# A vision tower's mixture-of-experts and linear-attention stages: GpSimd's order fixed by hand among the expert blocks and in the first attention units

## The chip, the cores and the metric

The kernel runs on one core of a Trainium2 chip. A core has a tensor engine for matrix products (PE, whose weight loads are a row of their own, PEld), a vector engine (DVE), a scalar engine (ACT), GpSimd (POOL) and a sync engine (SP) that issues most DMA transfers. Each engine executes its own list of instructions in order, and waits on semaphores for the others. The metric is the device time of one execution in microseconds, lower is better.

## The reference

The program is a two-layer transformer tower on 4 images. A tokenizer makes 784 tokens of 256 features from 8 x 8 patches, and three equal copies of them, so 3136 distinct tokens are computed and the output is written three times. Layer 0 has an attention across images and then a mixture of six experts, of which each token takes two:

```python
top_w, top_i = jax.lax.top_k(expert_logits, TOP_K)
routing_weights = jax.nn.softmax(top_w, axis=-1)
...
combined = jnp.sum(sel * routing_weights[..., None], axis=2)
```

Layer 1 has a linear attention. Its q and k come from normalised rows, and its sums run over all tokens of an image:

```python
k2 = _l2_normalize(k2 / (k2s + EPS_DIV), axis=-2)
q2 = _l2_normalize(q2 / (q2s + EPS_DIV), axis=-1)
kv = jnp.einsum('bnc,bnd->bcd', k2, v)
t2 = jnp.einsum('bnc,bcd->bnd', q2, kv) / math.sqrt(N)
attn = v + t2
return attn @ W_out + b_out
```

A second mixture of four experts ends the layer. Between the parts stand residual adds and layer norms.

## The kernel before, in words

The 3136 tokens lie as 25 tiles of 128 rows in a resident array `h`: six tiles for each image, and one last tile that holds the 16 remaining tokens of all four images (the remainder).

**Expert blocks.** The router has given every token two rows in a DRAM array, sorted by expert. The experts run over 30 blocks of 256 such rows: load a block, transpose it on PE, two hidden layers (`hidden`), the output layer (`rows_back`), and a write to the DRAM array `yrows`. Seven early blocks run beside the attention of layer 0; the loop at L1629 runs the other 23. A token's two results are fetched back from `yrows` by indirect DMAs on GpSimd, the gathers (`fetch`, L1531, the issue is L1540): one gather takes one of the two rows of each of 128 tokens, 128 KB.

**Units.** The linear attention works on units of three tiles: units 0 to 7, two for each image, and unit 8, `LU`, the remainder, with one tile. So `fetch` issues six gathers for a unit and two for the remainder. The gathered rows land in a buffer `ys`; units 0 to 7 share three buffers, and the remainder has one of its own. For each tile `stats_one` (L1548) adds the two rows, weighted, into `h` (L1554, two instructions) and takes mean and variance (`bn_stats` and `bn_aggr`, L1563 and L1564). Then `norm_root` (ACT) and `norm_rows` (DVE, L1585 and L1588) write the normalised rows `xa`, `x_t` transposes them on PE (L277), `qk_mm` makes q and k on PE (L1770), `qk_add` adds the bias (DVE, L1776), `qk_squares` takes the sums of squares (ACT), `root` and `factors` (DVE, L1808, L1809 and L1812) make the scales, `q_rows` (DVE, L1824) and `k_rows` (ACT, L1817) apply them, and `q_t` transposes q (PE, L277). When both units of an image are there, `k_x_tiles` (PE, L1869) and `k_x_left` (PE, L1876) sum k times x over the image's tiles and its part of the remainder, which is cut out of the remainder's normalised rows `xaL` into `xaM` by four GpSimd products (L1992). `rows_out` makes the output rows.

**What sets the order.** The kernel is written with a tile framework whose planner lays down each engine's list at build time. It goes by its own estimate of when an instruction's inputs will be there, and gives priority to what was written earlier. Inside a `manual_schedule` block the engines that are named keep the order in which the block is written. Instructions written outside the block may still be put between those of the block where the planner sees a gap. Before the change the block loop (L1627) fixes DVE and SP, and the block with the first units (L1974) fixes DVE, PE and ACT (`by_hand`); GpSimd is left to the planner in both. After the second block a loop over units 3 to 9 (L2055) is left to the planner altogether; there `q_k` (L1787) calls `stats_one` for the unit after the one whose q and k it makes. In the block loop the gathers of unit 0, unit 1, the remainder and unit 2 are written behind the block after which their rows are complete. Those of units 3, 4 and 5 are written in the second block, and the loop writes those of the unit three further on.

Of the kernel before, what the change touches and what calls it, by code (L numbers as in the profile page):

```python
# [65 lines left out]
def tile_vit_tower(ctx: ExitStack, tc: tile.TileContext, a: dict, out: bass.AP):  # L66
# [571 lines left out]
    ENG = mybir.EngineType  # L638
    by_hand = {ENG.DVE, ENG.PE, ENG.Activation}
# [575 lines left out]
    with tc.manual_schedule(engines=by_hand):  # L1215
        for s in range(NI - 1):
            u = (s - 1, 0, TPI) if s else None
# [62 lines left out]
    def load(i):  # L1280
        if i >= NBLK:
            return
        row = rowof[i] = nc.sync.value_load(meta(0, i), min_val=0, max_val=DUMMY)
        x = inT[i] = work[0].tile([P, 2, D], F32, tag="xb", name="xb", bufs=4)
        get = nc.sync.dma_start(
            out=x, in_=xrows[bass.ds(row, BLK), :].rearrange("(t p) d -> p t d", p=P)
        )
        if i < NEARLY:

            tc.declare_no_dep(get.ins, group="late scatter", reason="distinct rows")  # L1290
            tc.add_to_no_dep_group("early block", get.ins)
        for name in scatters[: scattered if i < NEARLY else None]:
            tc.add_manual_dep(
                get.ins, name,
                mybir.DependencyInfo(
                    mybir.DependencyClass.Sync, mybir.DependencyReason.DATA
                ),
                reason="rows scattered",
            )

    def own_weights(i):
        if i >= NBLK:
            return
        off = nc.vector.value_load(meta(1, i), min_val=0, max_val=(E0 - 1) * EW)
        w = own[i] = work[0].tile([P, EW], F32, tag="own", name="own", bufs=3)
        nc.vector.tensor_copy(w, ewf[0][:, bass.ds(off, EW)])  # L1306

    def turned(i):
        if i >= NBLK:
            return  # L1310
        x = inT.pop(i)
        pt = ps_tile("ptb").rearrange("p (c n) -> p c n", c=2)
        for c in range(2):
            for t in range(2):
                nc.tensor.transpose(  # L1315
                    pt[:, c, t * P : (t + 1) * P], x[:, t, c * P : (c + 1) * P], ident
                )
        xT = inT[i] = work[0].tile([P, 2, BLK], F32, tag="xTb", name="xTb")
        nc.scalar.copy(xT, pt)  # L1319

    def hidden(i, k):
        w = own[i]
        src = inT.pop(i) if k == 0 else h1s.pop(i)
        wm = w[:, k * 2 * D : (k + 1) * 2 * D].rearrange("p (c n) -> p c n", c=2)
        dst = work[0].tile([P, 2, BLK], F32, tag=f"hb{k}", name=f"hb{k}")
        for o in range(2):
            pm = ps_tile("pb")[:, :BLK]
            for c in range(2):
                nc.tensor.matmul(  # L1329
                    pm, wm[:, c, o * P : (o + 1) * P], src[:, c, :],  # L1330
                    start=(c == 0), stop=(c == 1),
                )
            b = w[:, 6 * D + 2 * k + o : 6 * D + 2 * k + o + 1]
            if o == 0 or i < NEARLY:
                nc.scalar.activation(dst[:, o, :], pm, AF.Relu, bias=b)  # L1335
            else:
                nc.vector.tensor_scalar(dst[:, o, :], pm, b, 0.0, ALU.add, ALU.max)  # L1337
        (hid2 if k else h1s)[i] = dst
# [25 lines left out]
    past, u, ua, ub = (s - 2, 0, TPI), (s - 1, 0, TPI), (s, 0, GT), (s, GT, TPI + 1 - GT)  # L1364
# [142 lines left out]
    LU = len(units)  # L1507
# [23 lines left out]
    def fetch(u):  # L1531

        if u >= len(units):
            return
        b, j0, n = units[u]
        y = ys[u] = own_of(lina, u, [TT, UT, 2, D], "ys", 3)
        for j in range(n):
            for k in range(2):
                t = b * TPI + j0 + j
                got = nc.gpsimd.indirect_dma_start(  # L1540
                    out=y[:, j, k, :], out_offset=None, in_=yrows[:, :],
                    in_offset=bass.IndirectOffsetOnAxis(ap=pos[:, k, t : t + 1], axis=0),
                )
                tc.add_to_no_dep_group("fetched", got.ins)
# [21 lines left out]
    def normalise(u):  # L1566
        norm_root(u)
        norm_rows(u)
# [55 lines left out]
        after[u] = NEARLY + most - 1  # L1624
    after[LU] = after[2] = NBLK - 1
    assert after[0] < after[1] < NBLK - 1
    with tc.manual_schedule(engines={mybir.EngineType.DVE, mybir.EngineType.SP}):  # L1627
        own_weights(NEARLY)
        turned(NEARLY)  # L1629
        for i in range(NEARLY, NBLK + 1):  # L1630
            if i < NBLK:
                load(i + 3)
                hidden(i, 0)
            rows_back(i - 1)
            own_weights(i + 1)
            turned(i + 1)
            if i < NBLK:
                hidden(i, 1)
            if i == NEARLY + 1:
                centred_weights()  # L1640
            for u in (0, 1, LU, 2):
                if i - 1 == after[u]:
                    fetch(u)

            for u, wait, two in ((0, 4, 1), (1, 4, 1)):
                j = (i - 1 - after[u] - wait) * two
                for k in range(j, j + two):
                    if 0 <= k < units[u][2]:
                        stats_one(u, k)
                    elif k == units[u][2]:  # L1650
                        normalise(u)
            if i - 1 == after[0] + 10:
                x_t(0)
# [317 lines left out]

    squares = {}
    steps = layer1_weights()
    with tc.manual_schedule(engines=by_hand):  # L1974
        x_t(1)
        for j in range(UT):
            qk_mm(0, j)
            qk_add(0, j)
            qk_squares(0, j)
        root(0)  # L1980
        for j in range(UT):
            qk_mm(1, j)
        qk_add(1, 0)
        qk_squares(1, 0)
        stats_one(LU, 0)
        norm_root(LU)
        factors(0)
        qk_add(1, 1)
        qk_squares(1, 1)
        norm_rows(LU)  # L1990
        for b in range(NI):
            nc.gpsimd.tensor_scalar(  # L1992
                xaM[:, b, :], xaL[:, 0, : D + 2], ofimage[:, b : b + 1], None, ALU.mult
            )
        fetch(3)
        fetch(4)
        qk_add(1, 2)
        qk_squares(1, 2)
        root(1)
        q_rows(0)  # L2000
        next(steps)
        x_t(LU)
        q_t(0)
        k_rows(0)
        next(steps)
        stats_one(2, 0)
        factors(1)
        q_rows(1)
        k_rows(1)
        qk_mm(LU, 0)  # L2010
        next(steps)
        Wvo, bvo = lw[:2]
        q_t(1)
        qk_add(LU, 0)
        qk_squares(LU, 0)
        root(LU)
        stats_one(2, 1)
        stats_one(2, 2)
        fetch(5)
        norm_root(2)  # L2020
        squares[0] = k_squares(0)
        factors(LU)
        fold(0, squares.pop(0))
        norm_rows(2)
        k_rows(LU)
        squares[LU] = k_squares(LU)
        q_rows(LU)
        squares[1] = k_squares(1)
        fold(1, squares.pop(1))
        k_x_tiles(0)  # L2030
        x_t(2)
        k_x_left(0)
        kn = k_norm(0)
        k_x_out(0, kn)
        qk_mm(2, 0)
        qk_add(2, 0)
        qk_squares(2, 0)
        stats_one(3, 0)
        qk_mm(2, 1)
        qk_add(2, 1)  # L2040
        qk_squares(2, 1)
        q_t(LU)
        gT = g_t(0)
        stats_one(3, 1)
        qk_mm(2, 2)
        qk_add(2, 2)
        kv_out(0, gT)
        qk_squares(2, 2)
        stats_one(3, 2)
        normalise(3)  # L2050
        rows_out(0)
        x_t(3)
    squares[2] = scales(2)
    fold(2, squares.pop(2))
    for u in range(3, LU + 2):  # L2055
        b, odd = divmod(u - 2, 2)
        one_image = not odd
        if u < LU:
            fetch(u + 3)
        if u == LU:  # L2060
            shared = shared1(0)
        if one_image:
            k_x(b)
            q_t(u - 1)
        if u < LU:
            q_k(u, 0, 2)
        if one_image:
            gT = g_t(b)
        if u < LU:
            q_k(u, 2, UT)  # L2070
            squares[u] = scales(u)
        if one_image:
            kv_out(b, gT)
        if u == LU - 1:
            rows_in(0)
            turn_rows(0)
            gate(0)
        if u < LU - 1:
            x_t(u + 1)
        if u == 3:  # L2080
            for k in pending:
                residual(k)
            pending = None
        rows_out(u - 2)
        if u == LU + 1:
            rows_left()
        if u < LU:
            fold(u, squares.pop(u))
            if u % 2:
                q_t(u - 1)  # L2090
# [103 lines left out]
```

## Time and profile before

| what | value |
|---|---|
| time, median of 3 runs | 788.0 us (787.89 to 788.85) |
| profiled execution: time, span | 788.72 us, 787.0 us |
| PE busy | 716.8 us, 91% of the span |
| DVE busy | 483.3 us, 61% |
| ACT busy | 331.8 us, 42% |
| POOL busy | 128.5 us, 16%, 226 instructions |
| gathers (L1540) | 52, mean 988 ns |
| xaM products (L1992) | 4, mean 1000 ns |
| mean granted PE clock | 0.962 |

Times in the trace are counted from the start of the span. The block loop ends at about 469 us, the block with the first units runs to about 540, and the loop over units from 3 on to about 620. The page shows each engine's busy time, the span in 40 slices, the chain of work that ended last, and the costliest groups of instructions with the idle time before them and what ended it. The trace can be asked for a table by stretch, for the waits, and for any engine's instructions in order of time. A row of such a timeline gives start, duration, engine, line, operation, output and inputs, and in brackets how long the engine had been idle and what released it.

### The profile page before, as it was taken

The page shows a single profiled execution, that of the slowest core. Times are in us where ns is not written, and L with a number is a line of the kernel's source. Part 1 is how long each engine was busy: PE and PEld are TensorE (multiplying, and loading weights), DVE is VectorE, ACT ScalarE, POOL GpSimd, SP SyncE. Part 2 cuts the span into 40 slices and gives each one's busy share as a digit, 9 for nine tenths or more (in the row PEclk, how much of TensorE's full clock was granted, in tenths as well). Part 3 has the DMA queues.
Part 4 walks back from the last instruction along what each step waited for, and adds up shares of the span by engine and source line. Part 5 has one row for each costly group of instructions (what it writes and reads, how often), then busy time and mean ns, then how long its engine had stood idle before and what let it go on. Part 6 is the DMA issues. An engine that isn't in the chain of part 4 may idle for free.

```text
span 787.0 us, 10609 instructions
## 1 busy us (share of the span) xinstructions
PE 716.8 (91%) x3408; PEld 495.9 (63%) x3408; DVE 483.3 (61%) x1515; ACT 331.8 (42%) x777; POOL 128.5 (16%) x226
## 2 busy tenths in 40 slices
PE   6899899999888789999999997379999999999996
PEld 4746555665555568878888883347776775554653
DVE  4676786769778745464456654579965654444441
ACT  0555776555574653422223225135445613222221
POOL 5300000000155127300113007860000000000000
PEclk9999999999999789999999999579999999999999
DMA  8399999000021944423344243230000003223333
GB/s 199 104 418 416 419 415 396 2 0 1 7 75 51 305 165 154 132 95 104 97 131 127 89 128 95 82 92 1 1 0 1 1 21 96 75 65 106 104 104 111
DMA packets 57749, 98.07 MB, mean 125 GB/s; under 512 B 6407, under 2 KB 47598, under 8 KB 57694
## 3 DMA queue, kind: packets, MB, share of 16 engines
q1 hardware_dynamic: 51184, 80.96, 29.4%
q0 software_dynamic: 5632, 14.58, 6.1%
q10 hardware_dynamic: 878, 1.86, 1.0%
q8 instruction: 27, 0.44, 0.2%
q14 instruction: 28, 0.23, 0.1%
HBM read 31.50 MB, written 65.88 MB: 124 GB/s over the span
## 4 chain that ended last, share of the span: by engine, by line
PE 70%; DVE 14%; ACT 5%; DMA 5%; POOL 3%; issue 2%; SPq 1%; DVEq 0%; ACTq 0%; POOLq 0%
PE pb L1329 13%; PE pyb L1346 6%; PE pe L286 6%; PE pqk L1770 5%; PE ps L286 4%; PE pt L277 4%; PE pkv L286 4%; PE pw L552 3%; PE pwp L297 3%; PE ps L2144 3%; PE pout L1944 3%; PE pout L1949 3%; PE pukx L1869 2%; DVE prod L815 2%; PE pe L2114 2%
## 5 line engine op out<-in xcount | busy, mean ns | idle before, releaser
L1039 POOL DMA_INDIRECT xrows<-xn,pos x50 | 54.6, 1091 | 242.4 <-ACT kq L790 186.2
L1540 POOL DMA_INDIRECT ys<-yrows,pos x52 | 51.4, 988 | 145.8 <-DMA yrows<-yb 131.0
L1329 PE MATMUL pb<-xTb,own 128*128 128x256 f32 x240 | 59.0, 390 | 3.4 <-DVE r L899 1.8
L1335 ACT ACTIVATE hb<-pb,own 128x256 f32<-128x256 f32 x74 | 35.0, 473 | 55.0 <-PE pb L1329 48.3
L1329 PE MATMUL pb<-hb,own 128*128 128x256 f32 x240 | 57.1, 380 | 0.3 <-DVE hb L1337 0.3
L1346 PE MATMUL pyb<-own,hb 128*128 128x256 f32 x240 | 57.1, 380 | 0.0
L1329 PEld LDWEIGHTS pb<-xTb,own 128*128 128x128 f32 x240 | 44.8, 195 | 11.6 <-issue 1.9
L1346 PEld LDWEIGHTS pyb<-own,hb 128*128 128x128 f32 x240 | 45.5, 190 | 6.3 <-DVE hb L1337 0.2
L1329 PEld LDWEIGHTS pb<-hb,own 128*128 128x128 f32 x240 | 43.5, 191 | 5.8 <-DVE hb L1337 0.7
L1770 PE MATMUL pqk<-Wqkv,lxT 128*128 128x512 f32 x100 | 46.9, 616 | 0.2 <-ACT lxT L86 0.2
L277 PE MATMUL pt<-ident,xn 128*128 128x128 f32 x200 | 34.5, 301 | 12.6 <-DVE xn L578 6.6
L286 PE MATMUL pe<-xT,eW 128*128 128x512 f32 (+1 forms) x112 | 46.0, 554 | 0.0
L1352 DVE TENSOR_TENSOR yb<-pyb,eb 128x512 f32<-128x512 f32 x30 | 20.7, 691 | 40.7 <-PE pyb L1346 40.7
L1319 ACT COPY xTb<-ptb 128x512 f32<-128x512 f32 x30 | 17.5, 583 | 63.4 <-PE ptb L1315 63.4
L277 PEld LDWEIGHTS pt<-ident,xn 128*128 128x128 f32 x200 | 25.3, 150 | 28.3 <-ACT xn L913 8.8
L552 PE MATMUL pw<-Wall,pT 128*128 128x512 f32 x96 | 42.6, 594 | 0.0
L1337 DVE TENSOR_SCALAR hb<-pb,own 128x256 f32<-128x256 f32 x46 | 22.2, 482 | 28.7 <-PE pb L1329 28.6
L1554 DVE SCALAR_TENSOR_TENSOR h<-ys,wk,h 128x256 f32<-128x256 f32 x50 | 23.5, 484 | 17.7 <-DMA ys<-yrows,pos 17.3
L815 DVE SCALAR_TENSOR_TENSOR prod<-kq 128x784 f32<-128x784 f32 x32 | 30.4, 972 | 6.0 <-ACT kq L1173 3.4
L286 PEld LDWEIGHTS pe<-xT,eW 128*128 128x128 f32 x112 | 20.3, 190 | 21.5 <-issue 16.5
L1784 ACT ACTIVATE qk<-qk 128x256 f32<-128x256 f32 x50 | 20.4, 408 | 28.4 <-DVE qk L1776 26.0
L1306 DVE COPY own<-ew 128x1540 f32 x30 | 29.0, 968 | 5.1 <-issue 1.6
(398 smaller groups left out, 1467.7 us busy)
## 6 DMA issues: line engine op xcount, KB each, us to landing
xrows<-nothing SPq DMA_DIRECT2D x22, 896.0 KB
yrows<-nothing SPq DMA_DIRECT2D x22, 896.0 KB
out_dram<-h SPq DMA_DIRECT2D x23, 384.0 KB
xb<-xrows SPq DMA_DIRECT2D x30, 256.0 KB
yrows<-yb SPq DMA_DIRECT2D x30, 256.0 KB
ew<-in_L_ffn_expert_w_dram SPq DMA_DIRECT2D x6, 768.0 KB
wb<-wd SPq DMA_DIRECT2D x16, 128.0 KB
img<-in_x_dram SPq DMA_DIRECT2D x2, 588.0 KB
```

The source lines that it names most:

```text
L277: nc.tensor.transpose(pt[:, j * TT : (j + 1) * TT], xn[:, j, c * P : (c + 1) * P], ident[:TT, :TT])
L286: nc.tensor.matmul(pm[: wcols.stop - wcols.start, :n], w[:, c, wcols], xT(c), start=(c == 0), stop=(c == chunks - 1),)
L297: nc.tensor.matmul(pm[:, i, :], xT(c, t), w[:, c, :], start=(c == 0), stop=(c == chunks - 1))
L552: nc.tensor.matmul(pm, pixels(c, tiles[j]), Wall[:, c, :], start=(c == 0), stop=(c == 1))
L815: nc.vector.scalar_tensor_tensor(prod, qTs[s][:, o, :], 1.0, kT[:, o, t * SEQ : (t + 1) * SEQ], ALU.mult, ALU.mult, accum_out=atts[s][:, o ...
L1039: put = nc.gpsimd.indirect_dma_start(out=xrows[:, :], out_offset=bass.IndirectOffsetOnAxis(ap=pos[:, k, t0 + j : t0 + j + 1], axis=0), in_ ...
L1306: nc.vector.tensor_copy(w, ewf[0][:, bass.ds(off, EW)])
L1329: nc.tensor.matmul(pm, wm[:, c, o * P : (o + 1) * P], src[:, c, :], start=(c == 0), stop=(c == 1),)
L1335: nc.scalar.activation(dst[:, o, :], pm, AF.Relu, bias=b)
L1346: nc.tensor.matmul(pm[:, t, :], src[:, c, t * P : (t + 1) * P], wm[:, c, :], start=(c == 0), stop=(c == 1),)
L1540: got = nc.gpsimd.indirect_dma_start(out=y[:, j, k, :], out_offset=None, in_=yrows[:, :], in_offset=bass.IndirectOffsetOnAxis(ap=pos[:, k, ...
L1770: nc.tensor.matmul(pqk, xTs[u][:, c, cut(j, 1)], Wqkv[:, c, : 2 * D], start=(c == 0), stop=(c == 1),)
```

## The change

Three places are edited. In the block loop GpSimd is added to the engines whose order is as written. In the block with the first units the same is done: there the order as written is the four xaM products, the gathers of units 3 and 4, and, after the adds of unit 2, those of unit 5. In the loop over units the condition for a fetch is now `u + 3 < LU` in place of `u < LU`. Before, the loop fetched units 6 and 7 at u = 3 and 4 and, at u = 5, unit 8, which is the remainder, a second time into a new buffer that nothing reads; at u = 6 and 7 `fetch` returned at once. After, it fetches units 6 and 7 alone.

```diff
-    with tc.manual_schedule(engines={mybir.EngineType.DVE, mybir.EngineType.SP}):
+    with tc.manual_schedule(engines={ENG.DVE, ENG.SP, ENG.Pool}):
         own_weights(NEARLY)
         turned(NEARLY)
         for i in range(NEARLY, NBLK + 1):
...
     squares = {}
     steps = layer1_weights()
-    with tc.manual_schedule(engines=by_hand):
+    with tc.manual_schedule(engines=by_hand | {ENG.Pool}):
         x_t(1)
         for j in range(UT):
             qk_mm(0, j)
...
     for u in range(3, LU + 2):
         b, odd = divmod(u - 2, 2)
         one_image = not odd
-        if u < LU:
+        if u + 3 < LU:
             fetch(u + 3)
```

## The prediction

> **What bounds the kernel now.** I read the page first. TensorE (PE) is busy 91% of the span, so only stretches where PE stands still can give time. The slices show two weak places; the one that this edit can reach is at slices 26 and 27, 511 to 551 us, where PE falls to 3 and 7 tenths. There the page's costliest groups name DVE line L1554 (it adds a gathered expert row into h) with 17.7 us of idle time ended by DMA, and GpSimd's (POOL's) gathers, L1540. The table by stretch gives the limits. Columns are length, then busy time of PE, weight load, DVE, ACT and POOL, then the granted PE clock:
>
> ```profile
> 488.00:504.40 16.40, 0.00 (x0) 0.00 (x1) 4.60 (x14) 1.31 (x3) 13.45 (x14) 0.62 0.28 80
> 517.20:522.00 4.80, 4.75 (x18) 3.87 (x18) 4.03 (x10) 0.61 (x2) 3.71 (x3) 0.50 0.30 82
> 540.00:572.00 32.00, 32.00 (x143) 23.80 (x142) 30.24 (x93) 16.01 (x59) 0.00 (x0) 1.00 0.01 2
> ```
>
> PE does nothing for 16.4 us and comes back at half clock; after 540 us it is full. The chain that ended last shows what holds it:
>
> ```profile
> 489.22 0.95 POOL ys L1540
> ...
> 491.46 3.95 POOL xaM L1992 x4
> ...
> 500.65 2.79 DMA ys<-yrows,pos
> 503.53 0.48 DVE h L1554
> 504.02 0.28 DVE qk L1824
> 504.43 1.56 PE pt L277 x6
> ```
>
> The path runs through GpSimd: gathers at a pace of 1.25 us (0.95 busy and 0.30 of issue), the four xaM products, more gathers, one landing of 2.8 us, a DVE add, the scaling of unit 1's q rows (L1824), PE. Whose gathers these are is in DVE's timeline:
>
> ```profile
> 483.70 0.47 DVE L1554 SCALAR_TENSOR_TENSOR h<-ys,wk,h 128x256 f32<-128x256 f32 x1
> 493.22 1.13 DVE L1554 SCALAR_TENSOR_TENSOR h<-ys,wk,h 128x256 f32<-128x256 f32 x2 [9.04 <-DMA ys<-yrows,pos]
> 498.48 0.49 DVE L1554 SCALAR_TENSOR_TENSOR h<-ys,wk,h 128x256 f32<-128x256 f32 x1 [4.13 <-DMA ys<-yrows,pos]
> ...
> 501.36 0.16 DVE L1809 SCALAR_TENSOR_TENSOR ss<-ss,s 128x3 f32<-128x3 f32 x1
> 502.17 0.48 DVE L1554 SCALAR_TENSOR_TENSOR h<-ys,wk,h 128x256 f32<-128x256 f32 x1 [0.66 <-DMA ys<-yrows,pos]
> 502.57 0.18 DVE L1812 RECIPROCAL ss<-ss 128x6 f32<-128x6 f32 x1
> 503.53 0.48 DVE L1554 SCALAR_TENSOR_TENSOR h<-ys,wk,h 128x256 f32<-128x256 f32 x1 [0.77 <-DMA ys<-yrows,pos]
> ```
>
> L1808, L1809 and L1812 are the three lines of `factors(1)`; as written no add stands between them. So the adds there are from the loop at L2055 (`stats_one(4, ...)`), which the planner moved up into the hand-written stretch. The waits fit one by one: each ends 2.7 to 2.9 us after a gather began, at 490.48 (the fifteenth since 472.83), then 495.57 to 500.65. By the order of instructions in the built program, which the trace's rows follow, before the xaM products run 2 gathers of the remainder, 6 of unit 2, 6 of unit 3 and 1 of unit 4; after them 5 of unit 4, the remainder again (2), and 18 of units 5 to 7. DVE, in order, waits for unit 4, which nothing needs before 540, with unit 1's factors and unit 2's statistics behind it.
>
> **The change, part by part.**
>
> Block loop, POOL fixed by hand: the gathers of units 0 and 1 already stand as written (first at 389.71 and 417.15, each batch released by the write of yrows). Unit 0's last lands about 399 (396.18 + 2.8), its first add is at 410.96; unit 1's lands at 426.6, used at 439.06. Cost nothing under 11 us of cover; without it a late gather would stop DVE, and with it the blocks.
>
> Second fetch of the remainder: two gathers, at 501.90 and 503.15, 2 x 1.25 = 2.5 us on POOL's queue. Units 5 to 7 stand behind them and start up to 2.5 us earlier.
>
> POOL fixed in the first units: xaM goes ahead of unit 3's six gathers and unit 4's first. Its input xaL is ready at 480.49; unit 2's last gather ends 481.72 + 0.95 = 482.67, so POOL does not wait. xaM 482.7 to 486.7, unit 3 from 486.8 to 494.1, unit 4 starts at 494.3 to 500.6: its first gather is 3.8 us later, its other five stand where they were (495.57 to 500.65). Unit 3 lands at 489.6 to 496 and is first added at 526.6: hidden by 30 us. xaM is used at 518.8. SP's queue is not touched.
>
> So the last landing for unit 4 stays at 503.5, and the gain must come from what no longer stands behind it on DVE. The planner, too, now has unit 4 six to seven gather places later. In its old list five gather places (first to last add after the xaM products, 493.7 to 503.5) cover ten DVE instructions. Unit 4's adds should slide by about 14 others: past the bn pair, `factors(1)`, three q rows, bvo, bres, lqT, qk of the remainder, to `stats_one(2, 1)`. Then q rows and PE's transposes and pukx products (504.43 to 512.8 in the trace) run from 487.5, inside the wait. Still behind the adds are the rest of unit 2's statistics and `norm_rows(2)`. That tail measured 512.17 (last bn_aggr) to 517.25 (PE on xa of unit 2), with 0.73 and 0.66 of gather wait in it and four adds of later units (1.9, of which I count half, since the rest ran beside ACT's squares): 5.1 - 1.4 - 1.0 = 2.7. New start: 503.5 + 0.5 add + 0.6 bn pair + 2.7 = 507.3 instead of 517.25: 10 us.
>
> From there to the next unit's pqk took 22.4 us (517.25 to 539.67), half of it at half clock. PE now idles from about 494 (487.5 + 0.7 + 5.4 at full clock) to 507, and the 4.4 us gap before 517.25 was enough to show a clock of 0.50 behind it, so I keep the 22.4. Eight adds of units 5 and 6 that ran before 517 come into it, 8 x 0.48 = 3.8 us on a DVE that is 87% busy there (19.9 of 22.8 us from 517.2 to 540); the same slide carries out at its end the six adds of units 6 and 7 that stood between 519 and 530, 2.9. Net 10 - 0.9 = 9.1. Waits for the gathers of units 6 and 7 may cost 0 to 3.8 (none, or three places of 1.25), and those gathers start 0 to 2.5 earlier, so 5.3 to 9.1; I take 8, nearer the upper end, because in the trace the waits after 517 come to one of 0.32 only.
>
> xaM beside a busy DVE: the one add that met it took 0.73 instead of 0.48, and one product 1.19 instead of 0.94, so 0.25 each, bounded by 0 and by four such meetings, 1 us. I take 0, inside the rounding. [...]
>
> Sum: 787.0 - 8 = 779.0 of span; the profiled execution took 788.72, 1.72 more than its span and 0.72 over the median 788.0. Against the median: 780.0.
>
> **The rivals.**
>
> The waits nearly vanish: the planner puts unit 4's adds behind `norm_rows(2)`. Then x of unit 2 is on PE when pukx ends, about 495, 22 us early, and the gathers, pacing on to 520, give back some 7 in later adds: 15 gained, 773. For it: POOL's order puts them late; against: unit 4's gathers still come within one unit of their old place.
>
> The order of DVE stays: unit 4's adds remain in front of the q rows. Then only the remainder's 2.5 us is left: 785.5. For it: five of the six gathers stand where they stood.
>
> Slower: DVE becomes the bound after 540. There it is busy 30.24 of 32 us with PE full. If the adds of units 5 to 7 that ran before 540 (14 x 0.485 = 6.8) and three bn pairs (1.7) move behind it, 8.5 - 1.8 idle = 6.7 us too much. With 2.5 gained upstream that is 792. It decides once more than 1.8 us plus the upstream gain (9.8 with the forecast's 8) moves. Against: unit 5's rows are due on PE only at 566.6.
>
> No change to measure: the fillers eat what the wait gives; within 1.6 us.
>
> **How the numbers follow.** Forecast (4 to 12 us gained, 8 likeliest) 0.47; waits vanish (12 to 21) 0.20; order stays (1.6 to 4) 0.15; no change 0.08; slower 0.10. About 0.2% (1.6 us) is what a measurement of this kernel can tell from none. Faster 0.82, same 0.08, slower 0.10. Range 768 to 787: it leaves out the slower case, half of no change, and the top of the second, 0.18. The likeliest case alone is 776 to 784.
>
> **What would show it.** Right: xaM near 483, 50 gathers, no L1554 between L1808 and L1812, PE's transposes of unit 1 near 488 instead of 504.43, the longest add wait now inside unit 2's statistics, xa of unit 2 on PE near 507. Wrong: adds waiting at the old place; x of unit 2 at 495; DVE full with PE waiting after 540; POOL waiting for xaL.

## The result, and the profile after

The changed kernel takes 783.72 us (median of 6 runs, 782.12 to 786.0). The kernel before took 788.31 us beside it (6 runs, 787.89 to 789.97). The ratio is 0.994, with a 95% interval of 0.992 to 0.996, so the change gains 4.6 us where 8 were forecast. The profiled execution took 786.0 us, with a span of 784.3.

Since executions differ by a microsecond or two in what comes earlier, the traces are compared on a clock that starts at the remainder's first gather (472.83 us in the trace of before, 474.53 after). All marks below are microseconds from there. "q" is PE's transposes of unit 1's q rows, "x of unit 2" and "x of unit 3" are PE's transposes of those units' normalised rows, and "end" is the end of the span.

| kernel | q | x of unit 2 | x of unit 3 | end | end minus x of unit 3 |
|---|---|---|---|---|---|
| before | 31.6 | 44.4 | 65.8 | 314.2 | 248.4 |
| after | 14.9 | 40.1 | 61.4 | 309.8 | 248.4 |

The q transposes came forward by 16.7 us, x of unit 2 by only 4.4, and the end by the same 4.4. PE's timeline of the changed kernel has both marks. Columns are start, duration, engine, line, operation, tiles, and in brackets the idle time ahead and what ended it:

```profile
489.40 0.92 PE L277 MATMUL pt<-ident,qk 128*128 128x128 f32 x6
490.15 5.39 PE L1869 MATMUL pukx<-xa,uk 128*128 128x258 f32 x24
514.59 1.76 PE L277 MATMUL pt<-ident,xa 128*128 128x128 f32 x6 [19.05 <-DVE xa L1588]
```

PE now does unit 1's work inside the former gap. Then it stands for 19.05 us, waiting for unit 2's rows from DVE. The table by stretch of the same kernel has this gap and the busy stretch behind it (length, then busy time of PE, weight load, DVE, ACT and POOL, then PE's granted clock):

```profile
504.00:517.00 13.00, 2.41 (x8) 1.95 (x9) 9.55 (x29) 4.18 (x13) 9.03 (x8) 0.50 0.26 76
...
540.00:572.00 32.00, 32.00 (x144) 24.04 (x143) 31.01 (x98) 15.98 (x60) 0.00 (x0) 1.00 0.01 2
```

PE is still full after 540 us, so DVE, at 31.01 of 32, did not become the bound there. What holds unit 2's rows stands in DVE's timeline of the changed kernel:

```profile
488.47 0.19 DVE L1812 RECIPROCAL ss<-ss 128x6 f32<-128x6 f32 x1
488.69 0.91 DVE L1824 TENSOR_SCALAR qk<-qk,ss 128x256 f32<-128x256 f32 x3
498.53 0.48 DVE L1554 SCALAR_TENSOR_TENSOR h<-ys,wk,h 128x256 f32<-128x256 f32 x1 [8.93 <-DMA ys<-yrows,pos]
...
504.90 0.48 DVE L1554 SCALAR_TENSOR_TENSOR h<-ys,wk,h 128x256 f32<-128x256 f32 x1
505.31 0.18 DVE L1564 BATCH_NORM_AGGREGATE mv<-st 128x2 f32<-128x6 f32 x1
505.40 0.45 DVE L1554 SCALAR_TENSOR_TENSOR h<-ys,wk,h 128x256 f32<-128x256 f32 x1
505.77 0.95 DVE L1603 TENSOR_TENSOR h<-h,bout 128x768 f32<-128x768 f32 x1
...
509.44 0.48 DVE L1554 SCALAR_TENSOR_TENSOR h<-ys,wk,h 128x256 f32<-128x256 f32 x1 [1.38 <-DMA ys<-yrows,pos]
510.65 0.48 DVE L1554 SCALAR_TENSOR_TENSOR h<-ys,wk,h 128x256 f32<-128x256 f32 x1 [0.66 <-DMA ys<-yrows,pos]
511.86 0.48 DVE L1554 SCALAR_TENSOR_TENSOR h<-ys,wk,h 128x256 f32<-128x256 f32 x1 [0.33 <-DMA ys<-yrows,pos]
513.73 0.48 DVE L1554 SCALAR_TENSOR_TENSOR h<-ys,wk,h 128x256 f32<-128x256 f32 x1 [0.96 <-DMA ys<-yrows,pos]
514.13 1.06 DVE L1588 TENSOR_SCALAR xa<-h,mv,rstd 128x256 f32<-128x256 f32 x3
```

The q rows (L1824) follow `factors(1)` (L1812 is its last line) with no add between. The long wait for unit 4's gathers comes behind them; unit 4's last add is at 504.90, that at 505.40 is unit 2's own. Four more adds with waits then stand in front of the rows of unit 2 (L1588). By the order of instructions in the built program these four belong to unit 5, whose rows reach PE only at 566.41 in the trace of before. Their waits come to 1.38 + 0.66 + 0.33 + 0.96 = 3.33 us. GpSimd's timeline of the changed kernel says why unit 5's gathers are not there earlier:

```profile
484.38 3.69 POOL L1992 TENSOR_SCALAR xaM<-xaL,ofimage 128x258 f32<-128x258 f32 x4
...
502.06 0.95 POOL L1540 DMA_INDIRECT ys<-yrows,pos  x1 [0.30 <-issue]
505.83 1.71 POOL L1540 DMA_INDIRECT ys<-yrows,pos  x1 [2.83 <-DVE h L1554]
507.84 0.95 POOL L1540 DMA_INDIRECT ys<-yrows,pos  x1 [0.30 <-issue]
```

The units share three buffers, and in the built program unit 5's rows go where unit 4's were. So GpSimd waits 2.83 us, until unit 4's last add (504.90 to 505.38) is done, before unit 5's first gather. The chain of the changed kernel runs through exactly these steps:

```profile
504.90 0.50 DVE h L1554
505.40 0.43 issue
505.83 1.71 POOL ys L1540
...
510.34 3.29 DMA ys<-yrows,pos
513.73 0.48 DVE h L1554
514.21 0.34 DVE xa L1588
514.59 1.76 PE pt L277 x6
```

### The profile page after: what moved, and what is told of

It reads as the page before. It is cut to its first block, busy times and chain, and to the rows that moved or that the text cites. A ratio compares the mean times of both kernels' runs of the same rounds, so it can differ in the third digit from the quotient of the medians.

```text
span 784.3 us, 10607 instructions
## 1 busy us (share of the span) xinstructions
PE 714.5 (91%) x3408; PEld 493.7 (63%) x3408; DVE 483.3 (62%) x1515; ACT 331.9 (42%) x777; POOL 127.5 (16%) x224
## 4 chain that ended last, share of the span: by engine, by line
PE 70%; DVE 14%; DMA 6%; ACT 5%; POOL 2%; issue 2%; SPq 1%; ACTq 0%; DVEq 0%
PE pb L1329 13%; PE pyb L1346 6%; PE pe L286 6%; PE pqk L1770 5%; PE ps L286 4%; PE pt L277 4%; PE pkv L286 4%; PE pw L552 3%; PE ps L2144 3%; PE pwp L297 3%; PE pout L1944 3%; PE pout L1949 3%; PE pukx L1869 2%; DVE oT L850 2%; DVE prod L815 2%
## 5 line engine op out<-in xcount | busy, mean ns | idle before, releaser
L286 PEld LDWEIGHTS pe<-xT,eW 128*128 128x128 f32 x112 | 20.2, 190 | 21.6 <-issue 16.5
L1554 DVE SCALAR_TENSOR_TENSOR h<-ys,wk,h 128x256 f32<-128x256 f32 x50 | 23.9, 488 | 14.1 <-DMA ys<-yrows,pos 13.7
L1770 PEld LDWEIGHTS pqk<-Wqkv,lxT 128*128 128x128 f32 x100 | 19.3, 200 | 20.7 <-issue 18.6
```

What stands on the lines that cost most here:

```text
L286: nc.tensor.matmul(pm[: wcols.stop - wcols.start, :n], w[:, c, wcols], xT(c), start=(c == 0), stop=(c == chunks - 1),)
L1554: nc.vector.scalar_tensor_tensor(h[:, t, :], ys[u][:, j, k, :], wk[:, k, t : t + 1], h[:, t, :], ALU.mult, ALU.add,)
L1770: nc.tensor.matmul(pqk, xTs[u][:, c, cut(j, 1)], Wqkv[:, c, : 2 * D], start=(c == 0), stop=(c == 1),)
```

## The experiments

They are labelled by letter and number. e5 to e8 ran on a chip where the kernel before took 788.38 us. e1 to e4, and f1 to f4, ran on two slower chips, where it took 804.5 and 804.26; each ratio is against the runs of before on the same chip. The ratio need not be the quotient of the two medians (f1: 0.9801 against 0.9777), so a step of some 0.002 between two ratios should not be read. Marks, where the trace gives them:

| kernel | q | x of unit 2 | x of unit 3 | end | end minus x of unit 3 |
|---|---|---|---|---|---|
| e1, second part alone | 17.7 | 41.6 | 70.4 | 318.7 | 248.3 |
| e2, third part alone | 31.5 | 44.8 | 65.8 | 314.1 | 248.3 |
| e3, first part alone | 31.6 | 44.7 | 73.0 | 321.3 | 248.3 |
| e4, xaM late | 27.9 | 42.4 | 64.2 | 312.6 | 248.4 |
| e5, the change again | 14.9 | 39.9 | 58.9 | 307.1 | 248.2 |
| e6, unit 5's adds kept back | 14.6 | 36.3 | 55.3 | 303.6 | 248.3 |
| e7, units 4 and 5 kept back | 14.9 | 23.7 | 43.8 | 292.3 | 248.5 |
| e8, 4 kept back, 5 to 7 further | 14.9 | 23.7 | 45.3 | 293.8 | 248.5 |
| f1, before with 4 and 5 kept back | 20.2 | 30.0 | 57.2 | 305.7 | 248.5 |
| f2, as e2 | 31.6 | 44.8 | 66.2 | 314.5 | 248.3 |
| f3, as e4 | 27.8 | 42.3 | 64.1 | 312.5 | 248.4 |
| f4, as e7 | 14.9 | 23.9 | 57.7 | 306.2 | 248.5 |

From x of unit 3 on, every one of them takes 248.2 to 248.5 us. Whatever a kernel wins or loses must therefore lie ahead of that mark.

### One part at a time: e1 to e3, and f2

e1 is the kernel before with the second part alone:

```diff
-    with tc.manual_schedule(engines=by_hand):
+    with tc.manual_schedule(engines=by_hand | {ENG.Pool}):
         x_t(1)
```

> Only the block with the first units fixes GpSimd's order; the block loop and the second fetch of the remainder stay as before. Theory: the whole gain is here, because the products xaM ahead of the gathers of units 3 and 4 let the planner put unit 4's adds behind unit 1's q rows; the remainder's two idle gathers fall into the 2.8 us for which POOL waits for unit 5's buffer. Expected 783.7 us, PE back on unit 1's q transposes about 15 us after the first gather of the remainder. Rival (the two gathers saved are the gain): 786 to 788.

Measured: 800.38 us (10 runs, 798.66 to 804.52), ratio 0.9949 (0.992 to 0.9979), the whole change's ratio. The marks are finer than that. x of unit 2 stands at 41.6, so this part alone brings 2.8 of the 4.4. The built program says where the rest is. With GpSimd's order fixed in this block, the planner no longer puts the remainder's second fetch behind unit 4's gathers, but ahead of the xaM products. GpSimd's timeline of e1, whose first gather is at 479.87, agrees:

```profile
492.24 3.70 POOL L1992 TENSOR_SCALAR xaM<-xaL,ofimage 128x258 f32<-128x258 f32 x4
```

That is a mark of 12.4, against 484.38 - 474.53 = 9.9 in the changed kernel: two gathers more, 2.5 us. Unit 4's last add is later by as much, and x of unit 2 by 1.6.

e2 is the third part alone, and f2 is the same kernel again on the other slow chip:

```diff
-        if u < LU:
+        if u + 3 < LU:
             fetch(u + 3)
```

> Only the second fetch of the remainder is left out. Theory: nothing, 788.0, because unit 5's first gather waited for unit 4's buffer at 504.4 anyway, so that POOL stands for 2.2 us where it issued the two gathers. Rival: the gathers of units 5 to 7 come 2.5 us earlier and the time falls by as much, 785.8.

> The third part alone once more, on another chip, since on the first one the profiles of four kernels had single stalls of 5 to 12 us on every engine that the profile puts to no engine of this core. Theory (the two gathers sat in the time in which GpSimd waits for unit 4's buffer; leaving them out saves nothing): 788.3 us, 0.998 to 1.002 of before, x of unit 2 on PE 44.4 to 44.8 us after the remainder's first gather. Rival A (they delay units 5 to 7 by 2.5 us): 785.8 us. Rival B (the 0.9% of the first chip was the kernel's): 781 us.

Measured: e2 798.87 us (10 runs, 793.21 to 802.77), ratio 0.9911 (0.9876 to 0.9946); f2 799.34 us (9 runs, 795.23 to 803.37), ratio 0.9933 (0.9906 to 0.996). e2's total misses both of its expectations, on the side of more gain. f2's misses the theory and rival A; rival B, 781 us, lies at the edge of its interval. Yet both traces have the marks of the profile of before to within 0.4 us all the way to the end. So no step that the trace shows was shortened. Why the two gathers' 2.5 us are not gained stands in e2's gathers (busy time and mean ns, then idle time and what ended it):

```profile
L1540 POOL DMA_INDIRECT ys<-yrows,pos x50 | 49.9, 998 | 148.7 <-DMA yrows<-yb 132.1 <-issue 13.9 <-DVE qk L1824 2.8
```

GpSimd waits 2.8 us for DVE in place of issuing them. Where the gain in the totals comes from is taken up in the part on the hardware, below.

e3 is the first part alone:

```diff
-    with tc.manual_schedule(engines={mybir.EngineType.DVE, mybir.EngineType.SP}):
+    with tc.manual_schedule(engines={ENG.DVE, ENG.SP, ENG.Pool}):
         own_weights(NEARLY)
```

> Only the block loop fixes GpSimd's order. Theory and rival alike: nothing, 788.3, gathers of units 0 and 1 at the same places.

Measured: 804.53 us (10 runs, 800.53 to 806.97), ratio 0.9989 (0.9963 to 1.0016). No difference, as expected, and there can be none: the built program is that of before, for every engine instruction for instruction, with the same waits. So e3's profile can stand for one of before on that slow chip.

### xaM behind the gathers: e4 and f3

The changed kernel, with the four xaM products written behind the gathers of units 3 and 4:

```diff
         norm_rows(LU)
+        fetch(3)
+        fetch(4)
         for b in range(NI):
             nc.gpsimd.tensor_scalar(
                 xaM[:, b, :], xaL[:, 0, : D + 2], ofimage[:, b : b + 1], None, ALU.mult
             )
-        fetch(3)
-        fetch(4)
```

> As after, but the four xaM products are written behind the gathers of units 3 and 4. Unit 4's gathers run 3.7 us earlier than in after. Theory: the planner then puts unit 4's adds in front of unit 1's q rows again, and DVE waits there; the last of them lands near 25 us after the first gather of the remainder in place of 28, and about 2.5 to 4 us are gained against before: 785. Rival (the landing of unit 4 decides, wherever its adds stand): earlier than after by 3.7, 780.

> The change with xaM behind the gathers of units 3 and 4, on another chip; DVE's order is that of before. On the first chip its x of unit 2 stood on PE 42.4 us after the remainder's first gather (before 44.4, the change 40.1), and its end 1.6 us nearer to that gather than before's. Theory (the gain is read from these marks): 786 to 787 us, 0.997 to 0.998. Rival A (the 1.4% of the first chip was the kernel's): 777 us. Rival B (no change of DVE's order, no gain): 788.3 us.

Measured: e4 794.59 us (4 runs, 792.67 to 797.18), ratio 0.9856 (0.9798 to 0.9913); f3 794.18 us (4 runs, 792.55 to 795.69), ratio 0.9861 (0.9825 to 0.9896). DVE's order is that of before, with unit 4's adds in front of the q rows. Unit 4's gathers now precede xaM, so the waits end earlier: q at 27.9 instead of 31.6, x of unit 2 at 42.4 instead of 44.4. By the marks this order gains 1.6 to 1.7 us. The ratio says 11, more than either theory, and most of that is again not in any step of these traces. So rival A of f3, which has the ratio right at 777, is not borne out by the marks. Nor is the rival of e4, whose 780 lies inside e4's interval: x of unit 2 is 2.3 us later than in the change, not 3.7 earlier. For the forecast it means this: moving xaM behind the gathers gives back 2.3 us of the 4.4 at x of unit 2, because the adds then go back to their old place in DVE's order.

### DVE's order: e5 to e8

Unit 5's adds can be kept behind `norm_rows(2)` on DVE by an order between two instructions of the same engine. e6 does this to the changed kernel; in its trace no add stands between the end of unit 2's statistics at 508.26 and the rows at 510.32, where the changed kernel has four:

```diff
-            nc.vector.scalar_tensor_tensor(
+            add = nc.vector.scalar_tensor_tensor(
                 h[:, t, :], ys[u][:, j, k, :], wk[:, k, t : t + 1], h[:, t, :],
                 ALU.mult, ALU.add,
             )
+            if u in HOLD:
+                tc.add_manual_dep(
+                    add.ins, normed_last[HOLD[u]],
+                    mybir.DependencyInfo(
+                        mybir.DependencyClass.NoSync, mybir.DependencyReason.DATA
+                    ),
+                    reason="adds later",
+                )
```

`normed_last[u]` is the last instruction of `norm_rows(u)`. HOLD names for a unit the unit whose rows must come first: `{5: 2}` in e6, `{4: 2, 5: 2}` in e7, `{4: 2, 5: 3, 6: 3, 7: 3}` in e8. e5 is the changed kernel itself, on the same chip.

> The changed kernel once more, beside the next three on one chip: 783.7.

> After, with unit 5 to come later: its adds may not be put in front of unit 2's normalised rows on DVE (an edge of order alone). Theory (four adds of unit 5 in front of these rows, with 3.3 us of gather waits, are what the forecast missed): x of unit 2 is on PE about 35 us after the first gather of the remainder, not 40, and the time falls by 4 to 5 us to 779. Rival (the stretch is held by DVE's own work or by PE's half clock): 783.

> As the run before, and unit 4's adds too stand behind unit 2's normalised rows. Theory (every wait of DVE in front of these rows is one for units that are not due): x of unit 2 on PE at 21 to 22 us after the first gather of the remainder, right behind the pukx products, PE stays at full clock, and some of it comes back as waits in the folds: 771. Rival (DVE's work has to be done before 540 anyway, DVE is the bound there): 778 to 780.

> Unit 4's adds behind unit 2's normalised rows, those of units 5 to 7 behind unit 3's. Theory: as the run before or up to 2 us better, 769 to 771, because fewer adds of later units stand in front of x of unit 3. Rival (units 5 to 7 come too late and DVE becomes the bound behind 540): 775 or more.

Measured against 788.38 us of before: e5 781.55 us (6 runs, 779.78 to 783.64), ratio 0.9913 (0.9884 to 0.9942); e6 778.48 us (4 runs, 777.19 to 779.82), ratio 0.9871 (0.9831 to 0.9911); e7 766.41 us (4 runs, 765.18 to 767.42), ratio 0.9726 (0.9685 to 0.9766); e8 768.29 us (4 runs, 764.24 to 769.95), ratio 0.9735 (0.9684 to 0.9785).

e5 came 2.2 us below its expectation (the last section has a possible reason). e6 is the test of the step that failed. With unit 5's adds out of the way, x of unit 2 comes at 36.3 instead of 39.9, and the time falls by 3.1 us against e5, somewhat less than the 4 to 5 expected. The theory holds in the main: unit 5's adds and their waits took back most of what the forecast had counted.

e7 takes away the wait for unit 4 as well. PE's timeline of e7, and DVE's waits for gathers (L1557 is its add line, since the edit shifts the lines), read:

```profile
495.29 1.31 PE L277 MATMUL pt<-ident,xa 128*128 128x128 f32 x6 [2.65 <-DVE xa L1599]
```

```profile
497.92 0.48 DVE L1557 SCALAR_TENSOR_TENSOR h<-ys,wk,h 128x256 f32<-128x256 f32 x1 [0.71 <-DMA ys<-yrows,pos]
...
501.64 0.48 DVE L1557 SCALAR_TENSOR_TENSOR h<-ys,wk,h 128x256 f32<-128x256 f32 x1 [0.83 <-DMA ys<-yrows,pos]
```

PE's gap of 19.05 us is 2.65 us here, and of 13.7 us of gather waits on DVE (the changed kernel, all 50 adds) two remain, together 1.54. In e7's built program unit 5's rows go where unit 2's were, so that GpSimd's wait of 2.8 us for the buffer, which e6 still has, is gone too. e7 beats both kernels, 15.1 us faster than the change and 22.0 faster than before. It also beats its expectation, which had some of the gain given back by gather waits further on; none came, as the constant 248 us behind x of unit 3 says. e8, which pushes units 5 to 7 further back still, is no better.

### Does GpSimd's order matter once DVE's is right: f1 and f4

f1 makes e7's edit to the kernel before, with none of the three parts; f4 is e7 again. DVE's list of instructions is the same in both. GpSimd's differs: in f1 xaM stands behind 15 gathers, in f4 behind 8, and f1 fetches the remainder twice.

> The kernel before, with all three parts of the change left out, and with one edit of another kind: the adds of units 4 and 5 are kept behind norm_rows(2) on DVE. DVE then has, instruction for instruction, the order of the version of the change that keeps both units' adds behind norm_rows(2) (766.4 us, 0.973 of before); only GpSimd's order is still that of before, xaM after the gathers and the remainder fetched twice. Theory (what the change gains is nothing but where DVE's adds of units 4 and 5 stand against norm_rows(2); GpSimd's order pays by that alone): 766 to 768 us, x of unit 2 on PE about 24 us after the remainder's first gather as there. xaM then ends 22.6 us after that gather, ahead of the matmuls that read it at 24.9, so its late place costs nothing. Rival A (xaM's early place is worth the change's own 4.6 us): 771 us. Rival B (with no adds in front, no gather waits for a buffer, and the second fetch's two gathers, 2.5 us, delay units 5 to 7): 769 us.

> The change with the adds of units 4 and 5 kept behind norm_rows(2), again, beside the kernel before with the same DVE order. Theory: 766.4 us, 0.973 of before, and equal to the kernel before with those adds kept back within 0.3%. Rival A: 4 to 5 us ahead of it, since xaM stands early. Rival B: 2.5 us ahead of it, for the two gathers.

Measured: f1 786.31 us (4 runs, 783.79 to 795.17), ratio 0.9801 (0.9746 to 0.9856); f4 785.2 us (4 runs, 782.6 to 789.0), ratio 0.9744 (0.9706 to 0.9782). f4 has e7's ratio. f1 and f4 lie 1.1 us apart by their medians, but 0.0057, some 4.6 us, by their ratios, whose intervals overlap. With four runs each and this scatter the totals can rule out neither rival A's 4 to 5 us nor rival B's 2.5. The marks speak against rival A: x of unit 2 is at 30.0 in f1, and 5.8 us of that is one DVE stall of the slow chip ahead of it (below), which f4 does not have; without it, it would be 24.2, as expected, against 23.9 in f4. What is shown is this: DVE's order alone, without any part of the change, gains about 2% there (1.4% at the least by the interval), where the change gained 0.6% and 0.9% on its two chips. Whether GpSimd's order is worth anything beside it is not settled, since f1 was not run on a chip without the stalls.

## Why the prediction came out as it did

The time forecast was 780.0 us and 783.72 came, inside the likeliest case's own 776 to 784. The direction and the mechanism were right. The size was not: 8 us forecast, 4.6 measured.

**Block loop, nothing.** Right: the built program does not change at all (e3).

**Second fetch, units 5 to 7 up to 2.5 us earlier.** Wrong. Unit 5's first gather is at a mark of 31.3, against 31.6 before. In the trace of before the last of the two superfluous gathers and unit 5's first are:

```profile
503.15 0.95 POOL L1540 DMA_INDIRECT ys<-yrows,pos  x1 [0.30 <-issue]
504.40 0.96 POOL L1540 DMA_INDIRECT ys<-yrows,pos  x1 [0.30 <-DVE qk L1824]
```

Unit 4's last add, which frees unit 5's buffer there too, ended at 503.53 + 0.48 = 504.01. So the two superfluous gathers filled time in which unit 5's could not have started; without them GpSimd waits 2.83 us. The forecast looked at the queue's pace and not at the buffer. The edit does have a worth, in another place: beside the second part it keeps the two gathers from standing ahead of xaM, which cost e1 1.6 us at x of unit 2.

**xaM ahead of units 3 and 4, unit 4's adds slide behind the q rows.** Right, nearly to the place. xaM starts at 484.38 (forecast on the old trace's clock 482.7, thus 484.4 on this one) and waits for nothing. The q transposes are at a mark of 14.9 (forecast 487.5 - 472.83 = 14.7). Unit 4's last add ends at 30.9 (forecast 31.2).

**The tail from there to x of unit 2, 0.5 + 0.6 + 2.7.** This is the step that failed. x of unit 2 was forecast at a mark of 507.3 - 472.83 = 34.5, and is at 40.1, 5.6 us later. From unit 4's last add to the end of unit 2's statistics 0.6 was forecast, and 2.6 measured (505.38 to 508.00): two of unit 2's own adds (0.45 and 0.48) and two additions of the output bias (L1603, 0.95 and 0.42) stand there, which in the old trace lay in the stretch between the q rows and the tail and were not carried over. From there to PE 2.7 was forecast, and 6.6 measured (508.00 to 514.59): the gather waits, set to nothing, are 3.33, and the half of four adds that was left out (1.0) is still there; the rest of the tail was 0.4 shorter. That is 2.0 and 3.9 too little, less 0.3 since unit 4's last add began that much earlier by the marks: 5.6. "Unit 4's adds slide" was right, but the adds of unit 5 stayed in front, and their gathers could not start before unit 4's last add had freed their buffer. e6 removes these adds and gets 3.6 us of it back at x of unit 2.

**22.4 us kept from there to the next pqk, 0.9 to 4.7 given back.** From x of unit 2 to unit 3's pqk (x of unit 3 and about one microsecond) it took 22.4 us in both profiles, and nothing was given back. The forecast's 2 us for this were too many, so by luck this error made good a part of the one before. In e5, the changed kernel again, the stretch took 20.0 us, so that the two profiles agree so closely is partly chance (the clock, below).

**xaM beside a busy DVE, 0.** Right in the total. Two adds met it and took 1.56 us together, where four took 1.66 at 502.82, so 0.73 more:

```profile
485.72 1.56 DVE L1554 SCALAR_TENSOR_TENSOR h<-ys,wk,h 128x256 f32<-128x256 f32 x2
```

They lie ahead of DVE's wait of 8.93 us, which hides them. xaM itself took 3.69 us against 3.95 before, and the three q rows began at 488.69, after xaM's end at 488.07, so GpSimd lost nothing.

**The rivals.** That the order of DVE stays is ruled out by the q rows at 488.69. DVE as the bound after 540 is ruled out by PE's 32.00 of 32.00. "The waits nearly vanish", 773, did not happen by the planner. Made by hand it is e7, and it is worth more than the 15 us that were put on it, since nothing was given back in later adds.

**Two readings.** Slices 26 and 27 of the page span 492 to 531 us, not 511 to 551, and x of unit 5 is on PE at 566.41, not 566.6. Neither enters the sum.

## What to carry to other kernels

An engine's wait for data that only later work needs can be costly for everything behind it on its list (here 8.93 us of DVE for unit 4, inside a gap of 19.05 us on PE), so ask of each wait not only when its data lands, but who stands behind it and whether that work needs the data. Where a list is laid down by a planner, move the consumer directly: e7's order on DVE is worth 22 us, while reordering the producers reached it only through the planner's estimates and brought 4.6 to 6.8. And before counting a removed transfer as time gained, look whether the next one waits for a free buffer, as unit 5's did here for 2.83 us. A part that leaves every engine's list as it was, like the first one here, is the same program, whatever its ratio says (0.9989 in e3).

## What was not expected of the hardware

**Single stalls on two chips.** The profiles from the chips where the kernel before takes 804 us have single stalls that the others lack, most of 5 to 12 us, on DVE, ACT or PE while gathers are in flight (0.68 MB of them in e3 from 529 to 536). Through ACT's stall in e3 GpSimd works on, with 0.30 or 0.31 us between gathers. The releaser of the engine that stalls first is given as "remote", or as plain "issue" (for DVE in e2 as PE's pbvo). ACT of e3, PE of e3, DVE of f1 and PE of f4:

```profile
536.05 0.48 ACT L86 COPY lxT<-pt 128x384 f32<-128x384 f32 x1 [11.79 <-remote]
```

```profile
536.59 5.17 PE L1770 MATMUL pqk<-Wqkv,lxT 128*128 128x512 f32 x8 [7.07 <-ACT lxT L86]
```

```profile
493.69 0.56 DVE L88 COPY lqT<-pt 128x384 f32<-128x384 f32 x1 [5.78 <-remote]
```

```profile
529.83 3.78 PE L1941 MATMUL pkvo<-Wvo,gT 128*128 128x256 f32 x8 [11.97 <-ACT gT L1932]
```

They explain the late marks: x of unit 3 at 73.0 in e3 and 70.4 in e1 (7 us each), 57.2 in f1 and 57.7 in f4 (13 to 14 each, against 43.8 in e7). e2, e4, f2 and f3 have none between the first gather and x of unit 3 that moves a mark. One stall comes back at the same instruction: ahead of the copy L88 in the row of f1 above, DVE stands some 5.8 us in e2, e3, e4, f1, f2 and f3, and not in f4. Where it moves no mark, a wait for unit 4's gathers follows it and takes it up (3.19 us of it left in e2). In f1 it moves x of unit 2. In e1 PE stands 2.96 us ahead of the q transposes, and q is at 17.7 and not at the 15 expected.

e3's program is that of before, so its profile shows what before does on that chip: PE's stall of 7.07 us, which e2 lacks, accounts for the 7.2 us between their ends (321.3 and 314.1). In these executions, then, e2 is ahead of before's program by a missing stall and not by a shorter step, and so is e4, but for its 1.6 us. For the second slow chip, which has no profile of before's program, this is only argued. Leaving out the second fetch may make the stall rarer: e2 and f2 took under 797 us in 7 of 19 executions, the program of before on these chips (e3's runs included) in none of 49. But f4, without the second fetch, has a stall as well. Neither what the stalls are nor what part the second fetch has in them was settled. The third part alone was not run on a chip without them.

**The clock behind the same gap differs from run to run.** Unit 2's pqk took 5.96 us for eight matmuls in the profile after and 3.68 in e5, the same kernel behind a gap of the same length (19.05 and 18.90 us). The granted clock over the 23 us that follow was 0.85 and 0.99:

```profile
517.00:540.00 23.00, 21.65 (x74) 13.90 (x73) 20.00 (x64) 8.62 (x33) 10.32 (x11) 0.85 0.23 63
```

```profile
515.00:538.00 23.00, 21.01 (x83) 13.27 (x82) 22.28 (x68) 10.46 (x42) 9.71 (x10) 0.99 0.22 63
```

x of unit 3 is 2.5 us earlier in e5 by the marks, and the eight matmuls are 2.3 of it. Why the clock differed behind gaps of the same length was not shown. The two medians of this kernel, 783.72 and 781.55, lie about as far apart as this one effect.
